# A two-layer graph attention kernel: the bias products taken out of the matrix engine, the biases added to stored rows, and one normalisation moved from VectorE to ScalarE

## The chip, the cores and the metric

The kernel runs on one core of one Trainium2 chip. The metric is the device time of one execution in microseconds (us); shorter is better. The core has five engines with a queue each: TensorE (PE in the profile, with its weight loads as PEld), VectorE (DVE), ScalarE (ACT), GpSimd (POOL) and SyncE (SP). Transfers are issued from the queues of SP, ACT and POOL and are carried by 16 DMA engines.

## The reference

A graph has 3125 nodes with 768 features and 53125 edges, sorted by destination (two directions of 25000 edges, and one loop per node). The reference adds one more loop per node inside each layer.

```
h  = relu(layernorm(x))
# layer 1: 4 heads of 256 columns
xl = h @ W1
e  = leaky_relu((xl . a_src)[src] + (xl . a_dst)[dst], 0.2);  alpha = softmax of e over the edges of one dst
g  = sum over edges (xl[src] * alpha) + b1
h1 = relu(layernorm(g) * g1 + be1) + (h @ Wr1 + br1)
# layer 2: one head of 768 columns
g  = sum over edges ((h1 @ W2)[src] * alpha2) + b2
out = x + layernorm(g) * g2 + be2 + (h1 @ Wr2 + br2)
```

The weights alpha of one node add up to 1. A vector added to every row of `xl` therefore comes out of the weighted sum unchanged.

## The kernel before

The nodes are cut into NB = 25 blocks of P = 125. The edges that end in one block fill a window of S = 2304 slots, J = 18 tiles of 128 slots. `in_order` (line 59) is the part that runs; `any_order` serves unsorted edges. The work has four stages.

**Stage 1, to about 515 us.** A loop over the blocks of x (line 683) does for each: `stats` (bn_stats on DVE, square root on ACT), `normal` (line 607, in place on the tile `xt`), `flip` (PE transposes, relu on ACT), and `fetch` of a later block of x into one of AHEAD = 8 `xt` tiles (line 590, from POOL's queue from block 4 on). Beside it run `edge_list`, `windows` and the folding of the attention vectors into W1 (lines 308 and 309), all on DVE. The generator `products` (line 637) multiplies each block by W1; ACT copies the two halves out of PSUM into `row` (line 648) and POOL's queue stores the row to `table1` (line 651). `split_biases` (line 155) splits b1, b2 and br2 + be2 into a high and a low part, and stores both in DRAM as `parts_d`. Then `softmax` (line 333) computes the weights of layer 1 for all windows: for each block it loads the destinations and sources of the window to all partitions (`bd`, `bs`, lines 370 and 372), turns them into one-hot matrices on DVE (`ohd`, `ohs`), picks rows by PE products, and reduces on DVE; steps of `products` fill PE between. What is left of `products`, and the first residual product (line 744), close the stage.

**Layer 1, to about 1511 us.** `sums` (line 486) goes through the blocks, 18 tiles each. For one tile, POOL gathers 128 rows of `table1` by an indirect DMA into `g` (line 525), one of ten buffers. In 17 of 18 tiles ACT writes `hi = g * alpha` rounded (line 543), DVE writes the remainder back into `g` (line 544), and PE multiplies both by a one-hot matrix made by DVE (lines 536 and 548) and adds up in the PSUM tile `pa`. In the remaining tile the weights go into the one-hot matrix, and PE works on full float32 (line 560). After the last tile of a block, two matmuls over two rows add the bias: `ones_r` by `b1_r`, high and low part (line 564); they are the last that write `pa`. Then `finish` (line 502) adds the row of the extra loop on DVE (line 512), and `end1` (line 793) runs spread over the next block's tiles: bn_stats, square root on ACT, normalisation on DVE (line 798), PE transposes, relu with g1 and be1 on ACT, the residual added on DVE, sixteen PE products with W2 (line 820), ACT copies the two halves of the row out of PSUM (line 824), DVE copies two attention columns (line 826), and SP stores the row to `table2`. The residual products of layer 1 (line 777) are spread between the tiles as well.

**The weights of layer 2, to about 1690 us.** `softmax` again, with `residual` (line 848) as filler on PE: sixteen products with Wr2 per block, then two matmuls that add br2 + be2 (line 858), then DVE adds the block of x (line 863). The first nine blocks are done here.

**Layer 2.** `sums` with one head of 768 columns and 18 buffers for `g`; 13 of 18 tiles are split, five use weights in the one-hot matrix. The two matmuls of line 564 add b2. The other 16 blocks of `residual` are spread over the tiles. `end2` normalises and adds, and ACT's queue stores the result.

The order on PE is as written in the source in all stages, that on ACT and DVE in stage 1's loop and in both calls of `sums`. Elsewhere, and on POOL and SP, a scheduler orders the instructions when the program is built. Each queue runs in its order, so an instruction that waits holds up what stands behind it.

The functions that the change touches, and what calls them:

Of the kernel before, what the change touches and what calls it, by code (L numbers as in the profile page):

```python
# [28 lines left out]
J = 18  # L29
# [29 lines left out]
def in_order(  # L59
# [45 lines left out]
    parts_d = dram.tile([2, HC + 2 * C2], F32, name="parts_d")  # L105
# [49 lines left out]
    def split_biases(pool):  # L155

        for name, vec, plus, n, o in (("b1", b1, None, HC, 0), ("b2", b2, None, C2, HC), ("ball", br2, be2, C2, HC + C2)):
            v = pool.tile([128, n // 128], F32, name=name + "_v")
            nc.sync.dma_start(v, vec.rearrange("(p c) -> p c", p=128))
            if plus is not None:  # L160
                u = pool.tile([128, n // 128], F32, name=name + "_u")
                nc.sync.dma_start(u, plus.rearrange("(p c) -> p c", p=128))
                nc.vector.tensor_add(v, v, u)
            hi = pool.tile([128, n // 128], F32R, name=name + "_hi")
            nc.vector.tensor_copy(hi, v)
            lo = pool.tile([128, n // 128], F32R, name=name + "_lo")
            nc.vector.tensor_sub(lo, v, hi.bitcast(F32))
            for i, t in enumerate((hi, lo)):
                nc.sync.dma_start(parts_d[i, o:o + n].rearrange("(p c) -> p c", p=128), t.bitcast(F32))

    def bias_rows(pool, o, n, name):
        t = pool.tile([2, n], F32R, name=name)
        nc.sync.dma_start(t.bitcast(F32), parts_d[:, o:o + n])
        return t

# [3 lines left out]
    def divided(pool, v, shape, name, by=P):  # L179

        t = pool.tile(shape, F32, name=name + "t")
        nc.vector.tensor_scalar(t, v, 1.0 / by, -0.5 + 0.5 / by, op0=OP.mult, op1=OP.add)
        ti = pool.tile(shape, I32, name=name + "i")
        nc.vector.tensor_copy(ti, t)
        q = pool.tile(shape, F32, name=name + "q")
# [3 lines left out]
        up = pool.tile(shape, F32, name=name + "u")  # L189
# [62 lines left out]
    def windows(pe):  # L252

        with tc.tile_pool(name="wn", bufs=1) as ep:
# [22 lines left out]
            q, _ = divided(ep, src_s, [128, NB * J], "sh")  # L277
# [55 lines left out]
    def softmax(heads, asad, al, alo_d, pp, nq, ends=False, scr=None, fill=iter(()), side=None,  # L333
# [8 lines left out]
        with tc.tile_pool(name="so", bufs=1, side=side, reuse_waits=waits) as so:  # L342
# [8 lines left out]
            with tc.tile_pool(name="sb", bufs=2, side=side, reuse_waits=waits) as sb:  # L351
# [16 lines left out]
                for b in range(NB):  # L368
# [3 lines left out]
                    bs = sb.tile([128, S], I16, name="bs", bufs=2)  # L372
# [6 lines left out]
                    ohs = sb.tile([128, S], BF16, name="ohs")  # L379
# [36 lines left out]
            with tc.tile_pool(name="sr", bufs=1, side=side, reuse_waits=waits) as sr:  # L416
# [5 lines left out]
                s = sr.tile([128, J, heads, NB], F32, name="s")  # L422
# [63 lines left out]
    def sums(heads, cols, table, al, alo_d, bias, split, ahead, his, lag, gp, pp, end, more=iter(())):  # L486
# [6 lines left out]
        assert split(0) or n == f  # L493
        running = []
# [21 lines left out]
        with tc.manual_schedule(engines={PE, ACT, DVE}) if lag else nullcontext():  # L516
            for b in range(NB):
# [3 lines left out]
                for j in range(J):  # L521
# [15 lines left out]
                    if split(j):  # L537
# [8 lines left out]
                        for t in (hi, g):  # L546
                            for i in range(2):
                                nc.tensor.matmul(pa[:, i, :f], oh[:, :P], t[:, i * f:(i + 1) * f],  # L548
                                                 start=(j == 0 and t is hi), stop=False)
# [12 lines left out]
                    if j == J - 1:  # L562
                        for i in range(2):
                            nc.tensor.matmul(pa[:, i, :f], ones_r, bias[:, i * f:(i + 1) * f],  # L564
                                             start=False, stop=True)
# [6 lines left out]
    with tc.tile_pool(name="m1", bufs=1) as mp:  # L572
# [10 lines left out]
        with tc.tile_pool(name="w1", bufs=1) as wp, tc.tile_pool(name="pm1", bufs=1, space=PSUM) as pm1:  # L583
            w1 = wp.tile([128, NK1, HC], F32, name="w1")
            wa1 = wp.tile([128, NK1, 2 * H], F32, name="wa1")
            h0 = []
            with tc.tile_pool(name="d1", bufs=2) as dp, tc.tile_pool(name="pd1", bufs=1, space=PSUM) as pp:
                xts = {}

# [47 lines left out]
                def products():  # L637

                    for b in range(NB):
                        gi, o = b // GB, (b % GB) * P  # L640
                        row = wp.tile([P, HC], F32, name="row", bufs=2)
                        for i in range(2):
                            pm = pm1.tile([128, 512], F32, name="pm", bufs=3)
                            for k in range(NK1):
                                nc.tensor.matmul(pm[:P], h0[gi][:, k, o:o + P], w1[:, k, i * 512:(i + 1) * 512],  # L645
                                                 start=(k == 0), stop=(k == NK1 - 1))
                                if k == NK1 - 1:
                                    nc.scalar.activation(row[:, i * 512:(i + 1) * 512], pm[:P], AF.Copy)  # L648
# [27 lines left out]
                with tc.manual_schedule(engines={ACT, DVE}):  # L676
# [6 lines left out]
                    for b in range(-2, NB + LAG):  # L683
                        if b + 2 < NB:
                            stats(b + 2)
                        if b == -1:

                            nc.vector.memset(w1[:, :, 0:HC:512], 0.0)
                            for i in range(2):
# [4 lines left out]
                                fetch(5 + 2 * i)  # L694
# [20 lines left out]
            with tc.tile_pool(name="pq1", bufs=1, space=PSUM) as pp:  # L715
# [6 lines left out]
                split_biases(mp)  # L722
# [27 lines left out]
        with tc.tile_pool(name="w2", bufs=1, reuse_waits="tile") as wp, tc.tile_pool(name="e1", bufs=2, reuse_waits="tile") as ep, \  # L750
# [12 lines left out]
            b1_r = bias_rows(wp, 0, HC, "b1_r")  # L763
# [29 lines left out]
            def end1(b, z):  # L793
# [4 lines left out]
                nc.vector.tensor_scalar(z, z, mu, rstd, op0=OP.subtract, op1=OP.mult)  # L798
# [30 lines left out]
            sums(H, C1, table1, al1, alo1_d, b1_r, lambda j: j % 18 != 8, 10, 4, 0, gp, pp, end1, later())  # L829


    with tc.tile_pool(name="m2", bufs=1, reuse_waits="tile") as mp, \
            tc.tile_pool(name="pr2", bufs=1, space=PSUM, reuse_waits="tile") as pr:
        al2 = mp.tile([128, J, 1, NB], F32, name="al2")
        ball_r = bias_rows(mp, HC + C2, C2, "ball_r")
# [4 lines left out]
        def load(b):  # L840
            if b < NB and b not in loaded:
# [58 lines left out]
        with tc.tile_pool(name="w3", bufs=1, reuse_waits="tile") as wp, tc.tile_pool(name="e2", bufs=2, reuse_waits="tile") as ep, \  # L900
                tc.tile_pool(name="g2", bufs=1, reuse_waits="tile") as gp, tc.tile_pool(name="pg2", bufs=1, space=PSUM, reuse_waits="tile") as pp:
            b2_r = bias_rows(wp, HC, C2, "b2_r")
# [12 lines left out]
            with tc.issue_after(behind):  # L915
                sums(1, C2, table2, al2, alo2_d, b2_r, lambda j: j % 18 not in (0, 4, 8, 12, 16), 18, 10, 5, gp, pp, end2, more)
# [472 lines left out]
```

## Time and profile before

| what | value |
|---|---|
| median of 15 executions | 2363.51 us (2354.13 to 2371.64) |
| the profiled execution's own time | 2368.95 us |
| its span, first to last instruction | 2367.1 us |
| mean granted PE clock | 0.974 |
| PE busy | 2213.1 us, 93% |
| DVE busy | 1975.8 us, 83% |
| ACT busy | 1295.1 us, 55% |
| POOL busy | 1197.3 us, 51% |
| moved by DMA | 637.97 MB, 270 GB/s on average |

The profile shows one execution. "Busy" counts an engine's time in instructions, waits left out. The span is also cut into 40 equal slices of some 59 us with the busy share of each in tenths. A group row gives line, engine, operation, output and inputs with their shapes, the count, busy us, the mean ns of one, and the idle time of the engine just before with what ended it. The chain of waits is followed back from the last instruction: at each step to what released it. A timeline row begins with start and length in us.

### The profile page before, as it was taken

The page shows a single profiled execution, that of the slowest core. Times are in us where ns is not written, and L with a number is a line of the kernel's source. Part 1 is how long each engine was busy: PE and PEld are TensorE (multiplying, and loading weights), DVE is VectorE, ACT ScalarE, POOL GpSimd, SP SyncE. Part 2 cuts the span into 40 slices and gives each one's busy share as a digit, 9 for nine tenths or more (in the row PEclk, how much of TensorE's full clock was granted, in tenths as well). Part 3 has the DMA queues.
Part 4 walks back from the last instruction along what each step waited for, and adds up shares of the span by engine and source line. Part 5 has one row for each costly group of instructions (what it writes and reads, how often), then busy time and mean ns, then how long its engine had stood idle before and what let it go on. Part 6 is the DMA issues. An engine that isn't in the chain of part 4 may idle for free.

```text
span 2367.1 us, 35889 instructions
## 1 busy us (share of the span) xinstructions
PE 2213.1 (93%) x11154; PEld 1436.0 (61%) x11154; DVE 1975.8 (83%) x4429; ACT 1295.1 (55%) x2687; POOL 1197.3 (51%) x1043
## 2 busy tenths in 40 slices
PE   5898999989999999999999999799999999999997
PEld 2566665436666666666666765476566666666664
DVE  6845999769999999898989999588678787778877
ACT  1222332229988888888888999100244444444443
POOL 2100000027765666655556776000377777777775
PEclk8898999989999999999999999899999999999999
DMA  5453552379998898988988998686499999898896
GB/s 185 147 190 103 182 192 87 112 237 376 336 324 304 288 340 296 314 314 287 332 289 295 335 319 291 243 292 236 157 316 331 331 321 316 312 310 309 299 308 226
DMA packets 185691, 637.97 MB, mean 270 GB/s; under 512 B 32170, under 2 KB 49435, under 8 KB 184724
## 3 DMA queue, kind: packets, MB, share of 16 engines
q0 software_dynamic: 109072, 437.23, 54.0%
q1 hardware_dynamic: 72570, 188.75, 22.7%
q10 hardware_dynamic: 3850, 9.60, 1.1%
q8 instruction: 93, 1.52, 0.2%
q14 instruction: 106, 0.87, 0.1%
HBM read 567.40 MB, written 68.08 MB: 268 GB/s over the span
## 4 chain that ended last, share of the span: by engine, by line
PE 59%; DVE 21%; DMA 12%; issue 3%; ACT 3%; POOL 1%; SPq 0%; ACTq 0%; DVEq 0%; POOLq 0%
PE pa L548 18%; PE p L820 10%; DMA g<-table,idx_s 9%; PE pr L777 7%; PE pr L854 6%; PE pm L645 5%; PE pa L560 5%; DVE g L544 5%; ACT hi L543 2%; DVE scr L394 2%; DVE al L397 2%; PE pq L392 2%; PE pm L744 2%; PE pas L633 1%; PE pa L564 1%
## 5 line engine op out<-in xcount | busy, mean ns | idle before, releaser
L525 POOL DMA_INDIRECT g<-table,idx_s x900 | 1088.9, 1210 | 485.8 <-PE pa L548 284.3
L543 ACT ACTIVATE hi<-g,al 128x256 fp32r<-128x256 f32 (+1 forms) x2025 | 1009.1, 575 | 469.8 <-DMA g<-table,idx_s 281.8
L544 DVE SCALAR_TENSOR_TENSOR g<-g,al,hi 128x256 fp32r<-128x256 f32 (+1 forms) x2025 | 1032.7, 560 | 131.9 <-ACT hi L543 130.3
L548 PE MATMUL pa<-hi,oh 128*125 128x512 f32 (+1 forms) x1500 | 602.8, 481 | 25.3 <-DVE oh L536 18.2
L548 PE MATMUL pa<-g,oh 128*125 128x512 f32 (+1 forms) x1500 | 473.8, 391 | 24.1 <-DVE g L544 23.8
L548 PEld LDWEIGHTS pa<-hi,oh 128*125 128x125 f32 x1500 | 273.6, 188 | 218.2 <-ACT hi L543 71.1
L548 PEld LDWEIGHTS pa<-g,oh 128*125 128x125 f32 x1500 | 270.8, 187 | 109.6 <-DVE g L544 67.4
L820 PE MATMUL p<-w,h1T 128*125 128x384 f32 (+1 forms) x800 | 299.9, 493 | 2.2 <-DVE h1T L811 1.9
L854 PE MATMUL pr<-wr,h 128*125 128x384 f32 x800 | 294.1, 500 | 3.8 <-DMA h<-h1T_d 3.2
L645 PE MATMUL pm<-w,h 128*125 128x512 f32 x600 | 283.7, 623 | 0.0
L777 PE MATMUL pr<-h0k,wr 128*128 128x500 f32 (+1 forms) x576 | 257.7, 536 | 10.3 <-DMA h0k<-h0T_d 10.2
L536 DVE TENSOR_SCALAR oh<-iota_f,rel_s 128x128 fp32r<-128x128 f32 x775 | 207.4, 279 | 60.3 <-PE pa L548 60.2
L560 PE MATMUL pa<-g,w 128*125 128x384 f32 (+1 forms) x700 | 235.0, 464 | 5.7 <-ACT w L558 4.8
L854 PEld LDWEIGHTS pr<-wr,h 128*125 128x125 f32 x800 | 149.8, 192 | 85.9 <-issue 13.5
L820 PEld LDWEIGHTS p<-w,h1T 128*125 128x125 f32 x800 | 148.4, 188 | 81.4 <-issue 10.9
L146 POOL DMA_DIRECT2D table<-row x25 | 15.8, 631 | 347.4 <-ACT row L648 320.4
L645 PEld LDWEIGHTS pm<-w,h 128*125 128x125 f32 x600 | 113.8, 197 | 126.7 <-issue 126.4
L560 PEld LDWEIGHTS pa<-g,w 128*125 128x125 f32 x700 | 129.2, 190 | 72.1 <-ACT w L558 15.0
L777 PEld LDWEIGHTS pr<-h0k,wr 128*128 128x128 f32 x576 | 104.5, 191 | 53.3 <-issue 11.5
L392 PEld LDWEIGHTS <-ohs 125*128 125x128 bf16 x2700 | 101.2, 98 | 48.3 <-DVE ohs L380 33.8
L392 PE MATMUL pq<-tabs,ohs 125*128 125x100 bf16 (+1 forms) x2700 | 104.9, 192 | 22.9 <-DVE ohs L380 21.1
L648 ACT ACTIVATE row<-pm 125x512 f32<-125x512 f32 x50 | 29.8, 595 | 150.9 <-PE pm L645 138.6
(198 smaller groups left out, 1681.8 us busy)
## 6 DMA issues: line engine op xcount, KB each, us to landing
bd<-dst_d SPq DMA_DIRECT2D x50, 576.0 KB
bs<-slo_d SPq DMA_DIRECT2D x50, 576.0 KB
g<-table,idx_s POOLq DMA_INDIRECT x900, 6.1
r1T_d<-rt SPq DMA_DIRECT2D x100, 125.0 KB
r1t<-r1T_d SPq DMA_DIRECT2D x25, 500.0 KB
h1T_d<-h1T SPq DMA_DIRECT2D x25, 500.0 KB
h<-h1T_d SPq DMA_DIRECT2D x25, 500.0 KB
own<-table SPq DMA_DIRECT2D x24, 512.0 KB
```

Of the source, the lines that this page charges most:

```text
L392: nc.tensor.matmul(q[:, j], ohs[:P, (j0 + j) * 128:(j0 + j + 1) * 128], tabs[:, i], start=(i == 0), stop=(i == 2))
L394: nc.vector.tensor_tensor(pick[:, j0:j0 + n], q, ohh[:, j0:j0 + n, None, :].to_broadcast([128, n, heads, NB]), OP.mult)
L525: nc.gpsimd.indirect_dma_start(out=gf, out_offset=None, in_=table[:, :], in_offset=bass.IndirectOffsetOnAxis(ap=idx_s[:, c:c + 1], axis=0))
L536: nc.vector.tensor_scalar(oh, iota_f, rel_s[:, c:c + 1], None, op0=OP.is_equal)
L543: nc.scalar.activation(hi[:, cs], gf[:, cs], AF.Copy, scale=a)
L544: nc.vector.scalar_tensor_tensor(g[:, cs], gf[:, cs], a, hi[:, cs].bitcast(F32), op0=OP.mult, op1=OP.subtract)
L548: nc.tensor.matmul(pa[:, i, :f], oh[:, :P], t[:, i * f:(i + 1) * f], start=(j == 0 and t is hi), stop=False)
L560: nc.tensor.matmul(pa[:, o // f, o % f:o % f + n], w[:, o // cols, :], gf[:, o:o + n], start=(j == 0), stop=False)
L645: nc.tensor.matmul(pm[:P], h0[gi][:, k, o:o + P], w1[:, k, i * 512:(i + 1) * 512], start=(k == 0), stop=(k == NK1 - 1))
L777: nc.tensor.matmul(pm[:, :nb * P], wr1[:, k, m * 128:(m + 1) * 128], loaded[gi, k][:, :nb * P], start=(k == 0), stop=(k == NK1 - 1))
L820: nc.tensor.matmul(pm[:, :n], hT[:, k, :], w2[:, k, o:o + n], start=(k == 0), stop=(k == NK2 - 1))
L854: nc.tensor.matmul(pm[:, :384], h1[:, k, :], wr2[:, k, i * 384:(i + 1) * 384], start=(k == 0), stop=False)
```

## The change

- The matmuls over two rows (lines 564 and 858), `split_biases`, `bias_rows` and the DRAM tensor `parts_d` go. The last product of a block carries the stop mark instead.
- b1 is added by GpSimd to each row of table 1 in SBUF, after ACT's copies and before the store.
- b2 is added by VectorE while it takes the row of table 2 out of PSUM; the two ScalarE copies there go.
- br2 + be2 is added by GpSimd to x, block by block, in stage 1 (`plus`); the sum is stored to DRAM as `xb_d`, and layer 2 loads it in place of x. `plus` reads `xt` before `normal` writes over it. b1, br2 and be2 are loaded, broadcast to 125 partitions, from ACT's queue.
- The normalisation of layer 1 (line 798) becomes an ACTIVATE with scale and bias; DVE makes the bias from mean and inverse deviation first.
- To make room: 7 `xt` tiles instead of 8; the one-hot matrix `ohs` is written over `bs`, of which there are 3 (layer 1) or 4 (layer 2) instead of 2; `s` is written over `m`; four tiles of a division share one.

```diff
-    parts_d = dram.tile([2, HC + 2 * C2], F32, name="parts_d")
+    xb_d = dram.tile([N, D], F32, name="xb_d")
...
-                    bs = sb.tile([128, S], I16, name="bs", bufs=2)
+                    bs = sb.tile([128, S], I16, name="bs", bufs=3 if scr else 4)
...
-                    ohs = sb.tile([128, S], BF16, name="ohs")
+                    ohs = bs.bitcast(BF16)
...
-                s = sr.tile([128, J, heads, NB], F32, name="s")
+                s = m
...
                                 nc.tensor.matmul(pa[:, i, :f], oh[:, :P], t[:, i * f:(i + 1) * f],
-                                                 start=(j == 0 and t is hi), stop=False)
+                                                 start=(j == 0 and t is hi),
+                                                 stop=(j == J - 1 and t is g))
...
-                    if j == J - 1:
-                        for i in range(2):
-                            nc.tensor.matmul(pa[:, i, :f], ones_r, bias[:, i * f:(i + 1) * f],
-                                             start=False, stop=True)
...
+            b1_b = wp.tile([P, HC], F32, name="b1_b")
+            nc.scalar.dma_start(b1_b, bcast(b1, HC))
...
+                ball_b = dp.tile([P, D], F32, name="ball_b", bufs=1)
+                nc.scalar.dma_start(ball_b, bcast(br2, D))
+
+                def plus(b):
+
+                    xb = dp.tile([P, D], F32, name="xb", bufs=XB)
+                    if b == 0:
+                        nc.scalar.dma_start(xb, bcast(be2, D))
+                        nc.gpsimd.tensor_add(ball_b, ball_b, xb)
+                    nc.gpsimd.tensor_add(xb, xts[b][:P], ball_b)
+                    store_rows(nc.gpsimd, xb_d, b, xb)
...
+                                        nc.gpsimd.tensor_add(row, row, b1_b)
                                         store_rows(nc.gpsimd, table1, b, row)
...
-                AHEAD, LAG = 8, 10
+                AHEAD, LAG, XB = 7, 10, 2
...
                         if 0 <= b + 1 < NB:
+                            if b == -1:
+                                plus(0)
+                                plus(1)
+                            if b + 3 < NB:
+                                plus(b + 3)
                             normal(b + 1)
...
-                split_biases(mp)
...
-            b1_r = bias_rows(wp, 0, HC, "b1_r")
+            b2_b = wp.tile([P, C2], F32, name="b2_b")
+            nc.sync.dma_start(b2_b, bcast(b2, C2))
...
-                nc.vector.tensor_scalar(z, z, mu, rstd, op0=OP.subtract, op1=OP.mult)
+                off = ep.tile([P, 1], F32, name="off")
+                nc.vector.tensor_scalar(off, mu, rstd, -1.0, op0=OP.mult, op1=OP.mult)
+                nc.scalar.activation(z, z, AF.Identity, bias=off, scale=rstd)
...
-                    nc.scalar.activation(row[:, o:o + 384], pm[:, :384], AF.Copy)
+
+                    nc.vector.tensor_add(row[:, o:o + 384], pm[:, :384], b2_b[:, o:o + 384])
...
-                load_rows(nc.sync, xr, x, b)
+                load_rows(nc.sync, xr, xb_d, b)
...
-                                     start=(k == 0), stop=False)
+                                     start=(k == 0), stop=(k == NK2 - 1))
                 yield
-            for i, pm in enumerate(pms):
-                nc.tensor.matmul(pm[:, :384], ones_r, ball_r[:, i * 384:(i + 1) * 384], start=False, stop=True)
```

More of the change, by code (lines that the diff above doesn't have):

```diff
@@ L153, in by_chunk, with divided @@
         return t
[L155 to L174, printed above, removed]
     def start_of(b):
         return nc.values_load(starts[0:1, b:b + 1], engines=[SP], min_val=0, max_val=E - S)
-    def divided(pool, v, shape, name, by=P):
-        t = pool.tile(shape, F32, name=name + "t")
+    def divided(pool, v, shape, name, by=P, room=None):
+        if room is None:
+            room = [pool.tile(shape, F32, name=name + x) for x in "tiqu"]
+        t, ti, q, up = room
+        ti = ti.bitcast(I32)
         nc.vector.tensor_scalar(t, v, 1.0 / by, -0.5 + 0.5 / by, op0=OP.mult, op1=OP.add)
-        ti = pool.tile(shape, I32, name=name + "i")
         nc.vector.tensor_copy(ti, t)
-        q = pool.tile(shape, F32, name=name + "q")
         nc.vector.tensor_copy(q, ti)
         nc.vector.scalar_tensor_tensor(t, q, -float(by), v, op0=OP.mult, op1=OP.add)
-        up = pool.tile(shape, F32, name=name + "u")
         nc.vector.tensor_scalar(up, t, float(by), None, op0=OP.is_ge)
@@ L276, in windows @@
             yield
-            q, _ = divided(ep, src_s, [128, NB * J], "sh")
+            room = ep.tile([128, 4, NB * J], F32, tag="tf", name="room")
+            q, _ = divided(ep, src_s, [128, NB * J], "sh", room=[room[:, i, :] for i in range(4)])
             nc.vector.tensor_copy(hi_s, q)
@@ L484, in softmax, with sums @@
         return behind
-    def sums(heads, cols, table, al, alo_d, bias, split, ahead, his, lag, gp, pp, end, more=iter(())):
+    def sums(heads, cols, table, al, alo_d, split, ahead, his, lag, gp, pp, end, more=iter(())):
         width = heads * cols
@@ L493, in sums @@
         assert split(0) or n == f
+        assert split(J - 1)
         running = []
@@ L693, in in_order @@
                                 fetch(4 + 2 * i)
-                                fetch(5 + 2 * i)
+                                if i == 0:
+                                    fetch(5)
                         if b == 1:
@@ L827, in end1 @@
                 store_rows(nc.sync, table2, b, row)
-            sums(H, C1, table1, al1, alo1_d, b1_r, lambda j: j % 18 != 8, 10, 4, 0, gp, pp, end1, later())
+            sums(H, C1, table1, al1, alo1_d, lambda j: j % 18 != 8, 10, 4, 0, gp, pp, end1, later())
     with tc.tile_pool(name="m2", bufs=1, reuse_waits="tile") as mp, \
@@ L834, in in_order @@
         al2 = mp.tile([128, J, 1, NB], F32, name="al2")
-        ball_r = bias_rows(mp, HC + C2, C2, "ball_r")
         FIRST = 9
@@ L901, in in_order @@
                 tc.tile_pool(name="g2", bufs=1, reuse_waits="tile") as gp, tc.tile_pool(name="pg2", bufs=1, space=PSUM, reuse_waits="tile") as pp:
-            b2_r = bias_rows(wp, HC, C2, "b2_r")
             g2_b = wp.tile([P, C2], F32, name="g2_b")
@@ L915, in in_order @@
             with tc.issue_after(behind):
-                sums(1, C2, table2, al2, alo2_d, b2_r, lambda j: j % 18 not in (0, 4, 8, 12, 16), 18, 10, 5, gp, pp, end2, more)
+                sums(1, C2, table2, al2, alo2_d, lambda j: j % 18 not in (0, 4, 8, 12, 16), 18, 10, 5, gp, pp, end2, more)
 @with_exitstack
```

## The prediction, on record before the result

> **What bounds the kernel now.** I read the slices first, then busy time by stretch, then the chain of waits in each stretch. A stretch row gives its length, busy us (and instructions) of PE, PEld, DVE, ACT and POOL, the granted clock, the DMA share and GB/s.
>
> ```profile
> PE   5898999989999999999999999799999999999997
> DVE  6845999769999999898989999588678787778877
> DMA  5453552379998898988988998686499999898896
> ...
> 40.00:100.00 60.00, 49.50 (x152) 25.12 (x152) 58.28 (x113) 13.44 (x34) 9.35 (x16) 0.89 0.38 125
> ...
> 300.00:385.00 85.00, 81.57 (x970) 54.03 (x971) 84.59 (x120) 29.42 (x31) 6.23 (x10) 1.00 0.50 161
> ...
> 600.00:800.00 200.00, 199.61 (x717) 129.08 (x716) 185.90 (x520) 173.40 (x433) 129.94 (x101) 1.00 0.90 315
> ...
> 1700.00:1900.00 200.00, 189.45 (x731) 129.50 (x731) 159.51 (x314) 94.64 (x108) 155.91 (x145) 0.99 0.92 320
> ```
>
> Four bounds follow each other. From 33 to 95 us and from 210 to 425 us DVE sets the pace (58.3 of 60, 84.6 of 85). In layer 1 it is PE (199.6 of 200), with DVE close behind at 93%. In layer 2 it is PE and the gathers in turn: between 1700 and 2300 us the chain of waits lies 29.5% on the gather's DMA and about 44% on PE (lines 548, 854, 560, 564), and ACT waits 248.0 us of 600 for gathered rows.
>
> **What goes from PE.** The price of a bias pair is read from starts, since matmul records overlap.
>
> ```profile
> 789.07 0.62 PE L548 MATMUL pa<-g,oh 128*125 128x512 f32 x2
> 789.54 1.45 PE L820 MATMUL p<-w,h1T 128*125 128x384 f32 x4
> ...
> 792.14 0.63 PE L548 MATMUL pa<-g,oh 128*125 128x512 f32 x2
> 792.70 0.72 PE L564 MATMUL pa<-b_r,ones_r 2*125 2x512 f32 x2
> 793.35 1.56 PE L820 MATMUL p<-w,h1T 128*125 128x384 f32 x4
> ```
>
> From line 548 to line 820 it takes 0.47 us without the pair and 1.21 with it: 0.74 us, 25 times, 18.5 us in layer 1. In layer 2 the same reading (1801.42 to 1802.39, against 1807.56 to 1807.91) gives 0.62 us: 25 pairs of line 564 are 15.5 us, 16 of line 858 are 9.9. In the second softmax line 854's four records and the pair take 2.02 us (1569.34 to 1571.36) against 1.33 for four records: 0.69 us, nine times, 6.2 us. Together 50.1 us; the two groups' busy time is 33.4 + 15.2 = 48.6, so the reading holds.
>
> **Layer 1: take -15.** A block takes 39.67 us (line 564 at 633.18 and 672.85) and PE is full, so up to 18.5 us come. DVE loses the normalisation (25 x 0.912 = 22.8) and gains 50 row adds out of PSUM at 546 ns (line 863, 125x384, same shape and places: 27.3) and 25 `off` at about 154 ns (line 327's reciprocal: 3.9): +8.4, or 0.33 a block. It then has 37.2 us of work in blocks of 38.9, 96%. ACT loses 24.6 (line 824) and gains 25 ACTIVATEs on 1024 elements, which I estimate at 1.03 us from 512 elements in 595 ns (line 648) and 2304 in 2123 (line 378): 25.8. New is a wait: ACT's normalisation waits for DVE's `off`, with the next tile's `hi` queued behind it, for which DVE and then PE wait. Four `hi` buffers lie between (ACT waits 71.0 us for PE from 560 to 1400, so they are mostly full). From 18.5 I take off 3.5 for this. If that cover fails, ACT's 1.03 us and DVE's 0.56 ahead of it come back in each block, and nothing is left.
>
> **Second softmax: -6.** PE is busy 84.8 of 87 us there, so nearly all comes; at worst, where DVE is last, nothing. `bs` no longer waits for DVE two blocks back but for PE's products four blocks back, long done; the order on SP is the same. I cost that at nothing; SP's row, if it did wait, would hold `bd` too.
>
> **Layer 2: -11.** Of 25.4 us only what lies on PE's part of the chain counts: 44% is 11. Ends: 0, if the DMA engines (0.92 busy) have no more to give, and 25. `xr` is loaded from `xb_d` instead of x, same size and queue.
>
> **Stage 1, its start: take +4.** DVE's queue stands still today for the split biases:
>
> ```profile
> 20.30 0.59 DVE L220 TENSOR_SCALAR_CACHE_REDUCE less<-d 125x425 bf16<-125x425 int16 x1
> ...
> 32.17 0.17 DVE L165 CAST b_hi<-b_v 128x8 fp32r<-128x8 f32 x1 [11.27 <-DMA b_v<-in_L_gnn_b_dram]
> ```
>
> This wait and some 1.0 us of small instructions go. What is late next: `normal` of block 0, today at 6.22 us, now waits for `plus(0)`, which in POOL's queue stands behind all twelve loads of W1 and another of x. Today these are issued by 20.7 us, each waiting for an earlier one to land. ACT's three broadcasts add 1.26 MB; at the 299 GB/s of the first 20 us that is 4.2 us. Then two GpSimd adds on 768 elements. Their price is in no row of this trace. POOL's select on 128x128 took 283 ns; in proportion to the elements 768 take 1.70 us and 1024 take 2.26, my upper end. DVE's TENSOR_TENSOR on 1024 took 1.217 us (line 308) and on 768 0.946 (line 736), my lower end. I take the upper, the row of the engine itself. So `normal(0)` starts near 20.7 + 4.2 + 3.4 = 28.3, DVE needs 10.3 us of work to the place where it stood, and 38.6 replaces 33.2 (32.17 and the 1.0): +5. Lower end, no delay of transfers and fast adds: 22.6 + 10.3 - 33.2 = -0.3. Upper end +8, if the adds are late again for the next blocks (two `xb` tiles, each bound to its store). I take +4.
>
> **Stage 1, GpSimd beside DVE: take +12.** 25 adds on 768 and 25 on 1024 elements come onto POOL, whose queue is nearly empty in time (9.4 us busy of the 60 shown), so their own time is hidden; the last lies under line 744's 40 us. But they may hold up DVE where it is the bound. A row shows that the two do meet:
>
> ```profile
> 285.77 1.19 POOL L146 DMA_DIRECT2D table<-row  x1 [18.32 <-ACT row L648]
> 286.04 0.80 DVE L375 TENSOR_SCALAR ohd<-bd,node_f 128x2304 bf16<-128x2304 int16 x1
> 286.95 0.51 POOL L147 DMA_DIRECT2D table<-row  x1
> ```
>
> An issue that takes 0.536 us in the median takes 1.19 beside a fast VectorE instruction. In DVE's two stretches stand about ten `plus` and four row adds, then eleven row adds: 10 x 1.70 + 15 x 2.26 = 51 us. Ends: 0, if they do not disturb DVE, and 51, if each stops it in full. DVE instructions with two SBUF operands or of the fast kind fill 46% of a folding round (2 x 1.22 + 0.62 of 6.69 us) and 41% of a softmax block (3.0 of 7.3), and part of each meeting falls on others: I take a quarter, 12 us.
>
> [...] The row above shows POOL as the loser; no row shows DVE losing. [...]
>
> **Sum.** -15 - 6 - 11 + 4 + 12 = -16, from the profiled execution's 2368.95 us (span 2367.1) to 2353. That execution lies 5.4 us above the median of 2363.5, so the same change to the median is 2347.5, my forecast.
>
> **Rivals.**
>
> - *The adds cost nothing.* For it: POOL is idle, and the wait of 11.27 us goes. Then -18.5 - 6.2, 60% of layer 2's 25.4 (-15) and 0: -40, 2324.
> - *The next engine takes over.* DVE at 96% and ACT's new wait keep layer 1 at -6, the gathers (0.92 of the DMA engines, 29.5% of the chain) keep layer 2 at -3, softmax -6, against +15: 2363.5, no change. Against it: the four `hi` buffers.
> - *GpSimd paces stage 1 (the slower one).* Place: DVE's stretches from 33 to 95 and 210 to 425 us. Price: 51 us in full. From a loss of 28 there, over half of each add, beside +4 and the gains of 32, the change stops paying. With 51 + 8 - 32 it is +27, 2390. For it: DVE has no slack there; against: most DVE time in the softmax goes to reductions and to instructions with an operand in PSUM.
>
> **Numbers.** Forecast 0.45 (own range 2335 to 2357), adds free 0.20, next engine 0.17, GpSimd as the bound 0.18. Faster by over 0.2% (4.7 us, what a measurement can tell from no change): 0.45 + 0.20 + 0.03 of the third = 0.68; same 0.14; slower 0.18. The range 2322 to 2372 takes in the first three and leaves out most of the last.
>
> **What would show it.** Layer 1's block of 39.67 us should come to 39.0; DVE near 95% there, and no longer PE waits for ACT. `normal(0)` should start at 26 to 30 us. Lines 308, 375, 380 and 382 should show longer or later instances beside POOL's adds; if the DVE-bound stretches keep their lengths, the quarter is wrong. Layer 2's blocks should shrink by 0.4 us of some 26; by 1.0 or by 0 the chain's shares misled me. The forecast fails if the adds last over 3 us, or ACT's wait for `off` empties the `hi` buffers.

## The result: slower by 2.8%, and the profile after

The changed kernel takes 2430.49 us (median of 9 executions, 2417.84 to 2436.3) against 2362.67 (47 executions): a ratio of 1.0278, with an interval of 1.0261 to 1.0295, and +68 us between the medians. Its profiled execution has 2421.39 us with a span of 2419.5, +52.4 to the span of before. The rest lies between executions: the profiled one is 9.1 us below its median, that of before 6.3 above.

The slices after, against those shown of before:

```profile
PE   2789888898899999999999998889899999998996
DVE  4983899877899999999999999767778878888887
DMA  6454454148999898899898989588289999998987
```

PE starts late (2 where there was 5), and the part up to layer 1 fills about one slice more. The stretches that answer to the four shown of before: folding, first softmax, layer 1, layer 2.

```profile
61.00:121.00 60.00, 45.87 (x130) 22.70 (x129) 58.11 (x76) 10.31 (x27) 41.01 (x40) 0.87 0.49 156
340.00:425.00 85.00, 75.27 (x872) 49.33 (x869) 85.00 (x109) 28.57 (x29) 15.32 (x12) 0.98 0.48 165
660.00:860.00 200.00, 195.45 (x696) 126.77 (x694) 183.97 (x524) 173.75 (x427) 139.13 (x104) 0.99 0.90 317
1750.00:1950.00 200.00, 183.06 (x701) 126.89 (x700) 155.97 (x307) 93.23 (x105) 155.62 (x145) 0.97 0.92 321
```

The first of these begins with the `pe<-cnt` product, which ends the start; the row of before at 40:100 begins 6 us ahead of it, among short instructions. From `pe<-cnt` on, before has:

```profile
46.10:106.10 60.00, 52.62 (x184) 28.63 (x185) 55.30 (x99) 13.73 (x35) 9.02 (x15) 0.87 0.42 139
```

In the first two, DVE is as full as before or fuller but gets less done: 76 instructions in 60 us where there were 99, 109 in 85 where there were 120. That is how a slowed engine looks: busy, with fewer and longer instructions. POOL went from 9.02 to 41.01 in the first.

Starts of the same instructions cut the span into stretches (us); the last ends with the last `z`. The other columns are experiments below, all from chips on which before took 2362 to 2367 us.

| stretch, to | before | after | e_no_plus | e_no_rowadd | e_neither | e_dma_b1 |
|---|---|---|---|---|---|---|
| `pe<-cnt` product | 46.1 | 60.7 | 51.5 | 59.9 | 45.6 | 37.5 |
| last folding reduction | 47.4 | 63.3 | 51.7 | 55.3 | 47.4 | 47.5 |
| first `pq` product | 115.3 | 124.1 | 113.7 | 117.9 | 115.7 | 118.5 |
| first scan | 187.6 | 201.2 | 201.4 | 186.1 | 186.3 | 190.4 |
| third scan | 29.7 | 34.6 | 34.6 | 30.0 | 29.7 | 30.3 |
| second softmax (layer 1) | 1086.8 | 1082.4 | 1078.9 | 1095.9 | 1095.5 | 1060.0 |
| its first scan | 126.8 | 132.0 | 128.4 | 131.7 | 126.1 | 125.5 |
| its third scan | 22.4 | 23.5 | 21.2 | 23.6 | 22.4 | 22.4 |
| last `z` (layer 2) | 699.2 | 691.9 | 697.7 | 694.5 | 694.8 | 699.1 |
| ratio to before | 1 | 1.0278 | 1.0105 | 1.0174 | 1.0036 | 0.988 |

Up to layer 1 the change loses 57.8 us (14.6 + 15.9 + 8.8 + 13.6 + 4.9); all after that gains 5.4, where the forecast had 32.

The start, in the timeline of after (POOL, then DVE):

```profile
29.29 0.54 POOL L140 DMA_DIRECT2D xt<-in_x_dram  x1 [1.02 <-DMA xt<-in_x_dram]
29.85 1.81 POOL L579 TENSOR_TENSOR ball_b<-ball_b,xb 125x768 f32<-125x768 f32 x1
31.74 3.56 POOL L580 TENSOR_TENSOR xb<-xt,ball_b 125x768 f32<-125x768 f32 x2
...
33.58 2.14 DVE L605 TENSOR_SCALAR xt<-xt,bn_mv,bn_rs 125x768 f32<-125x768 f32 x1 [23.00 <-POOL xb L580]
```

DVE's wait of 11.27 us went, and one of 23.00 came: the last load ahead of the adds is issued at 29.29. `normal` itself takes 2.14 us where it took 0.68 in before, with the second `plus` beside it.

The folding's products, as groups by line within their stretch, before and after:

```profile
L308 DVE TENSOR_TENSOR ab<-w,ab 128x1024 f32<-128x1024 f32 x12 | 14.6, 1217 | 0.0
```

```profile
L288 DVE TENSOR_TENSOR ab<-w,ab 128x1024 f32<-128x1024 f32 x12 | 26.3, 2192 | 0.0
L289 DVE TENSOR_REDUCE wa<-ab 128x4 f32<-128x1024 f32 x11 | 13.4, 1220 | 0.4
...
L580 POOL TENSOR_TENSOR xb<-xt,ball_b 125x768 f32<-125x768 f32 x8 | 17.4, 2181 | 0.1
L644 POOL TENSOR_TENSOR row<-row,b_b 125x1024 f32<-125x1024 f32 x3 | 8.2, 2736 | 15.7 <-ACT row L641 15.7
```

The twelve products with two SBUF operands take 11.7 us more, the reductions between them exactly what they took. DVE as a whole is not slower; some of its instructions are held. In the first softmax it is the three comparisons of 16-bit tiles, again before and after, from first `pq` to first scan:

```profile
L375 DVE TENSOR_SCALAR ohd<-bd,node_f 128x2304 bf16<-128x2304 int16 x23 | 18.5, 803 | 0.0
L380 DVE TENSOR_SCALAR ohs<-bs,node_f 128x2304 bf16<-128x2304 int16 x23 | 18.4, 802 | 0.0
L377 DVE TENSOR_SCALAR scr<-bd,node_f 128x2304 bf16<-128x2304 int16 x21 | 16.8, 801 | 0.0
```

```profile
L355 DVE TENSOR_SCALAR ohd<-bd,node_f 128x2304 bf16<-128x2304 int16 x23 | 26.4, 1147 | 0.0
L357 DVE TENSOR_SCALAR scr<-bd,node_f 128x2304 bf16<-128x2304 int16 x21 | 20.3, 966 | 0.0
L360 DVE TENSOR_SCALAR bs<-bs,node_f 128x2304 bf16<-128x2304 int16 x22 | 19.4, 884 | 0.0
...
L644 POOL TENSOR_TENSOR row<-row,b_b 125x1024 f32<-125x1024 f32 x9 | 24.2, 2685 | 161.1 <-ACT row L641 161.1
```

They take 66.1 us in place of 53.7: 12.4 of the stretch's +13.6. One meeting in the timeline of after:

```profile
261.60 2.34 POOL L644 TENSOR_TENSOR row<-row,b_b 125x1024 f32<-125x1024 f32 x1 [21.45 <-ACT row L641]
...
262.23 2.33 DVE L355 TENSOR_SCALAR ohd<-bd,node_f 128x2304 bf16<-128x2304 int16 x1
```

POOL's add ends at 263.94; `ohd` ends at 264.56, 0.62 us later. Alone it takes 0.80 us, so it got nearly nothing done beside the add. Each of the nine row adds of this stretch met such an instruction: four `ohd`, three `scr`, one `bs`, and one small instruction on `room` (2.22 us). The second scan of each pair loses 2.1 us (7.04 against 4.93), also beside a row add; before and after:

```profile
401.22 4.93 DVE L454 TENSOR_TENSOR_SCAN bw<-pen,scr 100x2304 f32<-100x2304 bf16 x1
...
454.12 7.04 DVE L435 TENSOR_TENSOR_SCAN bw<-pen,scr 100x2304 f32<-100x2304 bf16 x1
```

### The profile page after: what moved, and what is told of

The parts are those of the page before. It is cut to its first block, busy times and chain, and to the rows that moved or that the text cites. A ratio compares the mean times of both kernels' runs of the same rounds, so it can differ in the third digit from the quotient of the medians.

```text
span 2419.5 us, 35744 instructions
## 1 busy us (share of the span) xinstructions
PE 2189.8 (91%) x11004; PEld 1437.1 (59%) x11004; DVE 2037.8 (84%) x4472; ACT 1299.1 (54%) x2662; POOL 1367.3 (57%) x1144
## 4 chain that ended last, share of the span: by engine, by line
PE 54%; DVE 23%; DMA 14%; issue 4%; ACT 3%; POOL 1%; SPq 1%; ACTq 0%; DVEq 0%; POOLq 0%
PE pa L530 17%; DMA g<-table,idx_s 10%; PE p L822 9%; PE pr L777 7%; PE pr L856 5%; PE pm L638 5%; DVE g L526 5%; PE pa L543 4%; ACT hi L525 2%; DVE scr L374 2%; DVE al L377 2%; PE pm L743 2%; PE pq L372 2%; PE pas L626 1%; DVE z L494 1%
## 5 line engine op out<-in xcount | busy, mean ns | idle before, releaser
L507 POOL DMA_INDIRECT g<-table,idx_s x900 | 1111.8, 1235 | 460.2 <-PE pa L530 243.8
L530 PE MATMUL pa<-g,oh 128*125 128x512 f32 (+1 forms) x1500 | 485.6, 397 | 32.0 <-DVE g L526 31.4
L638 PE MATMUL pm<-w,h 128*125 128x512 f32 x600 | 291.0, 636 | 0.0
L644 POOL TENSOR_TENSOR row<-row,b_b 125x1024 f32<-125x1024 f32 x25 | 66.9, 2677 | 285.8 <-ACT row L641 285.8
L372 PEld LDWEIGHTS <-bs 125*128 125x128 bf16 x2700 | 102.4, 98 | 62.3 <-DVE bs L360 47.9
L372 PE MATMUL pq<-tabs,bs 125*128 125x100 bf16 (+1 forms) x2700 | 106.3, 193 | 35.4 <-DVE bs L360 32.6
L641 ACT ACTIVATE row<-pm 125x512 f32<-125x512 f32 x50 | 29.8, 596 | 187.4 <-PE pm L638 161.0
```

The lines of the kernel that those rows point to most:

```text
L372: nc.tensor.matmul(q[:, j], ohs[:P, (j0 + j) * 128:(j0 + j + 1) * 128], tabs[:, i], start=(i == 0), stop=(i == 2))
L507: nc.gpsimd.indirect_dma_start(out=gf, out_offset=None, in_=table[:, :], in_offset=bass.IndirectOffsetOnAxis(ap=idx_s[:, c:c + 1], axis=0))
L644: nc.gpsimd.tensor_add(row, row, b1_b)
```

## The experiments

**Theory:** GpSimd's adds hold up DVE where DVE sets the pace, and `plus` makes the start late. **Rival:** the changed rooms (`ohs` over `bs`, `s` in `m`, seven `xt`) slow stage 1. The chips are not alike: before took 2362 to 2413 us on them, with layer 2 alone 30 to 40 us longer on the slower ones, and layer 1 differs between them too. So each kernel is compared with runs of before on its own chip, by the ratio; the stretches on DVE agree between chips (folding 47.4 us in each kernel without adds).

**The parts undone one by one.**

```diff
-  nc.gpsimd.tensor_add(xb, xts[b][:P], ball_b); store_rows(nc.gpsimd, xb_d, b, xb)   # e_no_plus, e_neither
+  ball_r pair in residual(), xr from x
-  nc.gpsimd.tensor_add(row, row, b1_b)                                               # e_no_rowadd, e_neither
+  b1_r pair in layer 1
```

Where a pair comes back, so does the split of its bias at the start, and DVE's wait for it (10.9 us in `e_no_plus`, 10.7 in `e_neither`, 24.5 in `e_no_rowadd`, where `plus` stands at the start too).

> The changed kernel, but br2 + be2 are not added to x by GpSimd: they come back as the bias pair in the second softmax (hi and lo split on VectorE, two columns into the product), and xr is loaded from x. The row adds of b1 stay. Theory 1 (GpSimd's adds hold VectorE up, and plus(0) makes the start late): the 14.6 us of the late start and the 15.9 us that the folding stretch lost come back, less up to 6 us for the pair in the second softmax: 2395 to 2408 us, and the VectorE group of line 288 (2192 ns mean in the changed kernel, 1217 before) falls to below 1.4 us in its instances before 95 us. Rival (the shared buffers, the shorter list of fetches and the s = m room slow stage 1): 2425 to 2437.

Ratio 1.0105 (1.0069 to 1.0141), 2386.71 us: more came back than expected (1.7%). The folding took 51.7 us, its twelve products 1462 ns each, a little above the 1.4 expected: three row adds still stand beside them.

> The changed kernel, but b1 is not added to the rows by GpSimd: it comes back as the bias pair in layer 1's 25 blocks. plus stays. Theory 1 (GpSimd's adds hold VectorE up): the softmax loop's +16 us and the folding rounds' share of it go, but up to 18.5 us for 25 pairs come back in layer 1, of which the changed kernel gained only 6: 2405 to 2422 us, with the first softmax's blocks at 5.8 to 8.0 us and no ohd instance above 1.3 us between 245 and 440 us. Rival (the rooms): 2430 to 2450, the softmax's blocks stay uneven.

Ratio 1.0174 (1.0126 to 1.0221); 2407.07 us, as expected. Softmax and scans are back at 186.1 and 30.0, and the longest `ohd` takes 0.90 us where it took 2.92; layer 1 is at 1095.9, with the pair and the rest of the change.

> The changed kernel without either GpSimd add: b1 and br2 + be2 are bias pairs again; b2 on VectorE out of PSUM, layer 1's normalisation on ScalarE and all rooms stay as changed. Theory 1: stage 1 is as long as before the change (last reduction of the first softmax at 380 to 390 us), layer 2 keeps its 6 us or more: 2350 to 2362 us. Rival (the rooms slow stage 1): 2385 to 2415.

Ratio 1.0036 (1.0019 to 1.0053); 2374.65 us, 13 above the theory's upper end, on a chip where before took 2367.18. Stage 1 is as before in each stretch, as expected, but layer 1 is 8.7 us longer and layer 2 only 4.4 shorter. So of the 2.8% the adds cost 2.4, net of the pairs that they save and of the wait for their split, and the remaining parts of the change do not pay either.

> The kernel before with the changed rooms alone: bs with 3 or 4 buffers, ohs written over bs, s in the room of m, seven xt tiles in place of eight and the fetch of tile 5 alone moved; all bias products as before. Theory 1: 2360 to 2367 us, no change. Rival (the rooms slow stage 1): 2385 to 2420.

Ratio 0.9998 (0.9981 to 1.0015). The rival falls.

**What about the adds costs: their place, the rows' longer way, or SBUF?** On `e_neither`, an add or a set that touches no row:

```diff
+  nc.gpsimd.tensor_add(pad, pad, pad)   # e_scratch_add; e_scratch_set: nc.gpsimd.memset(pad, 1.0)
   store_rows(nc.gpsimd, table1, b, row)
```

> The kernel without GpSimd adds (e_neither, 2374.7 us), but at the place of each row add GpSimd adds a tile of 125 x 1024 of its own to itself: no one waits for it but the row's store behind it in POOL's queue, and it touches no row. The computation is otherwise that of e_neither. [...] Rival A, the cost is that of the row's way (ScalarE's row held longer by the add, its store later): 2370 to 2379, stretch 185 to 188.

If the adds' reads are what costs, the price was to be 15 to 25 us over `e_neither`, in the softmax stretch (first `pq` product to first scan, the stretch of these expectations), which would take 198 to 203. Ratio 1.0150 (1.0116 to 1.0184) against 1.0036, some 27 us: about that price, but not in that place. As nothing tied the adds to their rows, the scheduler put 23 of them into the folding, which grew from 47.4 to 71.2 us, while the softmax stretch stayed at 185.7. The groups within the folding:

```profile
L309 DVE TENSOR_TENSOR ab<-w,ab 128x1024 f32<-128x1024 f32 x12 | 27.0, 2250 | 0.0
...
L617 DVE TENSOR_SCALAR xt<-xt,bn_mv,bn_rs 125x768 f32<-125x768 f32 x7 | 10.8, 1540 | 0.3
...
L656 POOL TENSOR_TENSOR pad<-pad 125x1024 f32<-125x1024 f32 x23 | 51.6, 2243 | 1.4
```

Of the 23.8 us, the products took 12.4. `normal` took 6.0 (1.54 us in the mean where 0.68 is usual), so an instruction on float32 with one SBUF tensor is held as well.

> The same, but GpSimd sets its own 125 x 1024 tile to a constant: it writes SBUF and reads nothing. Theory 1 with the narrow rule (only reads meet VectorE's second operand; a write meets only the fast forms): 2374 to 2382 us, the stretch at 186 to 191, and the TENSOR_TENSOR group with two SBUF inputs (ohh, 1.5 us) unchanged beside a set while ohd and ohs may be longer. Rival B, any use of SBUF by GpSimd holds VectorE up: per microsecond of GpSimd as dear as e_scratch_add.

Ratio 1.0058 (1.0035 to 1.0081), folding 48.6 us (`ohh`, put at 1.5 us in the expectation, takes 0.61 in before). The same place, POOL writing only:

```profile
L309 DVE TENSOR_TENSOR ab<-w,ab 128x1024 f32<-128x1024 f32 x12 | 14.6, 1214 | 0.0
...
L656 POOL MEMSET pad<- 125x1024 f32 x24 | 23.8, 993 | 1.0
```

No data passes between the two engines in either kernel; 51.6 us of adds that read cost 23.8 us, 23.8 us of writes 1.2. An add alone takes 1.90 us here, so each cost DVE 1.03 us, 54% of it.

The softmax stretch had still to be tried with the row's way kept and its reads taken away:

```diff
-  nc.gpsimd.tensor_add(row, row, b1_b)
+  nc.gpsimd.memset(row, 1.0); nc.gpsimd.memset(row, 1.0)   # on e_no_plus
```

> The changed kernel with br2 + be2 as a bias pair (e_no_plus, 1.0105 of before), and at each row add's place GpSimd sets the row twice to a constant instead of adding b1: it waits for the row, holds it about 1.9 us and delays its store as the add (2.34 us) does, but reads no SBUF. The table of layer 1 then holds a constant, so the outputs are not the reference's. [...] Rival A (the row's longer way and its late store): stretch 198 to 202, ratio 1.008 to 1.011.

If only the adds' reads cost, the stretch to the first scan was to come back to 186 to 189 us, the scans' to 30 and the ratio to 1.000 to 1.003. Ratio 1.0015 (0.9998 to 1.0032), and the scans are back at 30.6; but the stretch to the first scan took 194.9, between that and the rival's. Its groups:

```profile
L381 DVE TENSOR_SCALAR bs<-bs,node_f 128x2304 bf16<-128x2304 int16 x22 | 21.7, 985 | 0.0
L376 DVE TENSOR_SCALAR ohd<-bd,node_f 128x2304 bf16<-128x2304 int16 x23 | 19.4, 846 | 0.0
L378 DVE TENSOR_SCALAR scr<-bd,node_f 128x2304 bf16<-128x2304 int16 x21 | 19.0, 904 | 0.0
```

The comparisons take 60.1 us, 6.4 above before, of +7.3 for the stretch. So the row's way without reads costs half of the 13.6, and most of that is again time in which DVE's comparisons are held. A set holds up the 16-bit comparisons too (0.85 to 0.99 us in the mean beside sets, 0.80 in before), though not products with two SBUF operands: they take 1214 ns beside sets (`e_scratch_set`), 2250 beside adds (`e_scratch_add`) and 1217 in before.

**The start.**

```diff
+  plus(0); plus(1)                 # ahead of W1's twelve loads in POOL's queue
   nc.gpsimd.dma_start(w1[...], W1[...])
```

> The changed kernel (2430.5 us) with plus(0) and plus(1) ahead of W1's twelve loads in POOL's queue, and the broadcast of b1 behind those of br2 and be2. Theory 2, the late start is the wait behind W1's loads: normal(0) moves from 33.6 us to about 14 to 18, the product pe<-cnt from 60.7 to 48 to 52, and 8 to 13 us of the whole go: 2417 to 2423. If the adds themselves and not their place make the start late: 2426 to 2433, normal(0) above 26 us.

Ratio 1.0250 (1.0214 to 1.0285), not told apart from the change's. `normal(0)` moved to 26.8 only, and `pe<-cnt` came at 64.6, later than in after. DVE's timeline:

```profile
26.80 2.14 DVE L605 TENSOR_SCALAR xt<-xt,bn_mv,bn_rs 125x768 f32<-125x768 f32 x1 [16.13 <-POOL xb L580]
...
42.73 2.15 DVE L605 TENSOR_SCALAR xt<-xt,bn_mv,bn_rs 125x768 f32<-125x768 f32 x1 [9.59 <-POOL xb L580]
```

23.00 us of waiting became 16.13 + 9.59: with the adds first, the first waits for the broadcast of be2 (landed at 22.6), and the third `plus` stands behind W1. The theory's figures fail; `normal(0)` above 26 us, as the other side had it, holds. The wait belongs to a chain of load, add and in-place `normal`, not to one place in the queue.

**The parts of layer 1 alone, on before.**

```diff
-  nc.scalar.activation(row[:, o:o + 384], pm[:, :384], AF.Copy)             # e_b2_only, and no b2_r pair
+  nc.vector.tensor_add(row[:, o:o + 384], pm[:, :384], b2_b[:, o:o + 384])
-  nc.vector.tensor_scalar(z, z, mu, rstd, op0=OP.subtract, op1=OP.mult)     # e_norm_only
+  nc.scalar.activation(z, z, AF.Identity, bias=off, scale=rstd)
```

> The kernel before with one part of the change: b2 is added by VectorE as it takes the rows for layer 2 out of PSUM, b2's pair in layer 2 goes. Normalisation stays on VectorE, b1 and br2 + be2 stay bias pairs. e_neither was 8.7 us longer than before from the scans to the last product of layer 1 and 4.5 shorter in layer 2. If VectorE's 50 row adds (27 us onto an engine at 93%) cost layer 1 that: layer 1 +6 to +15 here and the whole 2368 to 2378 us. If ScalarE's normalisation, which now waits for VectorE's off, costs it: layer 1 within 3 us of before, the whole 2358 to 2364.

Ratio 1.0067 (1.0043 to 1.0090): against before on the same chip, b2 on VectorE loses, although its pair in layer 2 is gone. Where is less clear. From the first to the last `z`, layer 1 takes 942.3 us, where before takes 931.3 on another chip. But `e_scratch_set`, on the chip of `e_b2_only`, takes 942.2 where `e_neither`, with the same layer 1, takes 933.9 on another. So these 11.0 us cannot be put down to the row adds. A block takes 39.7 us (median) in both kernels.

> The kernel before with one part of the change: layer 1's normalisation on ScalarE with VectorE's off, all biases as before. If VectorE's row adds alone cost layer 1 its +8.7 us, this takes 25 x 0.76 us off VectorE and leaves layer 1 (second pair of scans to the last product) at 1080 to 1088 us: ratio 0.996 to 1.001. If ScalarE's wait for off costs: layer 1 at 1090 to 1096, ratio 1.002 to 1.005.

Ratio 0.9993 (0.9974 to 1.0011): by itself it is worth nothing. First to last `z` take 932.5 us, against 929.6 on the same chip in `e_early_bias` below, whose layer 1 is that of before. Both parts together cost little between the first and the last `z`: on one chip, 933.9 in `e_neither` against 932.1 in `e_rooms`. Of the 10.0 us by which layer 1 is longer in `e_neither` than in `e_rooms`, 6.2 lie ahead of the first `z`, where no row add has run yet. From the third scan to the first `z`, nine of ten kernels with b2 on VectorE take 135 to 139 us (one takes 131), the five without 123 to 133. The broadcast of b2 (375 KB) now stands among layer 1's loads in SP's queue; whether it is the cause was not tried.

**The second softmax.** In after, `keep` is late, and in SP's queue g2's broadcast of 375 KB now stands ahead of it (SP and DVE, before and after):

```profile
1632.69 0.28 SPq L424 DMA_DIRECT2D keep<-keep_d  x1
...
1633.33 0.26 SPq L904 DMA_DIRECT2D g_b<-in_L_gnn_g_dram  x1
...
1638.80 0.75 DVE L426 TENSOR_SCALAR pen<-keep 25x2306 bf16<-25x2306 bf16 x1 [0.58 <-DMA keep<-keep_d]
```

```profile
1686.24 0.33 SPq L903 DMA_DIRECT2D g_b<-in_L_gnn_g_dram  x1
1687.58 0.27 SPq L405 DMA_DIRECT2D keep<-keep_d  x1
...
1697.31 0.75 DVE L407 TENSOR_SCALAR pen<-keep 25x2306 bf16<-25x2306 bf16 x1 [4.84 <-DMA keep<-keep_d]
```

```diff
-  nc.sync.dma_start(keep, keep_d[:R, :])
+  (nc.scalar if side else nc.sync).dma_start(keep, keep_d[:R, :])
```

> The changed kernel with one line moved: in the second softmax, keep is loaded from ScalarE's queue and no longer stands in SP's queue behind g2's broadcast. If that place is what made VectorE wait 4.84 us for keep ahead of the second softmax's scans: the wait falls below 1.5 us, first pq product to first scan of the second softmax from 132.0 to 127 to 129, ratio 1.024 to 1.027. If the DMA engines' load is the cause and not the queue: wait above 3 us, ratio 1.026 to 1.030.

Ratio 1.0224 (1.0197 to 1.0252); the wait fell to 2.81 us, but the stretch took 136.5, where three kernels with the pair took 129.8 to 133.9 on that chip. ScalarE issued `keep` only at 1694.54, after g2's broadcast (1690.46), so the edit did not bring the load forward: inconclusive.

The kept profiles say more of the order. The load of b2's vector, which stood between the two in before, does not decide it: `e_no_plus`, `e_neither`, `e_b2_only` and three more kernels have no such load either, and there `keep` is first and DVE does not wait for it. Of the kernels that load `keep` from SP's queue, g2 stands first only in after, `e_no_rowadd` and `e_plus_first`, all with `plus` and `xb_d`; there DVE waits 4.84, 5.44 and 0.95 us. On one chip the stretch to the first scan takes 131.7 in `e_no_rowadd`, and 128.4 and 126.1 in `e_no_plus` and `e_neither`. So `plus` is what goes with the late `keep`; that the order in the queue makes the wait is likely but not shown.

**A version that beats both.**

```diff
-  nc.sync.dma_start(v, vec.rearrange("(p c) -> p c", p=128))      # e_early_bias, on before
+  nc.scalar.dma_start(v, vec.rearrange("(p c) -> p c", p=128))
...
+  store_rows(nc.sync, table1, b, b1_b)                            # e_dma_b1: b1 into all rows first,
+  nc.gpsimd.dma_start(table1[rows of b], row, accum_op=OP.add)    # the row added on the way; no b1_r
```

> The kernel before with one line moved: the four loads of b1, b2, br2 and be2 for the split go to ScalarE's queue, ahead of its first work, in place of SP's queue behind the edge list's store. VectorE's wait of 11.27 us at 20.9 us goes, as the change promised it, and nothing is added to GpSimd. If VectorE's order is the bound from there on: pe<-cnt moves from 46 to 35 to 38 us and the whole loses 5 to 11 us, ratio 0.995 to 0.998. If W1's or x's loads are late next: pe<-cnt 40 to 45, ratio 0.998 to 1.001.

Ratio 0.9950 (0.9932 to 0.9967): `pe<-cnt` at 33.4, below the expected 35. This is the gain that the change was to have at the start, without `plus`.

> e_early_bias (ratio 0.995) with b1 in the table's rows as the change has it, but not by GpSimd's arithmetic: the table is first filled with b1's broadcast by 25 stores, and the rows' stores from POOL's queue add to what lies there in the DMA itself; layer 1's 25 pairs go; the changed rooms, b2 and br2 + be2 as before the change. If the loss in stage 1 was GpSimd's operand reads and the gain of b1's pair in layer 1 is real: fold 47 us, first pq product to first scan 186 to 188, first to last product of layer 1 shorter by 11 to 16 us than with the pair (941 to 948 in place of 951.7 from the second scans' first p product on), ratio 0.988 to 0.991. If the adding stores slow the stage (their read and write of HBM, the fill's 12.8 MB): ratio 0.993 to 1.003 with the stage's lengths up. If the layer gives the pair's time back to VectorE or the gathers: 0.994 to 0.996.

Ratio 0.9880 (0.9860 to 0.9900), 2336.33 us against 2362.20: the fastest of all. The folding stays at 47.5; the softmax stretch, at 190.4, is 2.4 above the expected. From first to last `z` layer 1 takes 914.9 in place of 931.3 (-16.4), a block 38.8. These two profiles need not be of one chip; on one chip `e_no_plus`, without b1's pair, takes 918.1, and `e_neither`, with it, 933.9: -15.8. Another 9.9 us come before the first `z`, where PE waited 10.2 us for the reloaded `h0k` and now waits 1.5; why these land sooner was not tried. POOL only issues; its groups in the softmax stretch:

```profile
L655 POOL DMA_DIRECT2D table<-row x9 | 11.3, 1259 | 0.0
L654 POOL DMA_DIRECT2D table<-row x9 | 9.8, 1089 | 170.2 <-ACT row L651 170.2
```

## Why the prediction was wrong

The forecast was 2347.5, 16 us below the median of 2363.5; the median became 2430.49, 67 above. The third rival, GpSimd as the bound, happened, given 0.18. Even its 2390 was too low, because it kept the gains of 32 us, of which 5.4 came.

- **GpSimd beside DVE, +12: the step that failed** is "part of each meeting falls on others: I take a quarter". No row of before shows which of DVE's instructions an add holds: that it is those in the 46% and the 41%, and the quarter, were the author's estimates. In after the folding's products (1217 to 2192 ns in the mean), the comparisons (0.80 to between 0.88 and 1.15 us), `normal` in the folding (0.68 to 0.86) and the second scan (4.93 to 7.04) were held, the reductions (1220 ns) were not. In the two stretches that it counted, folding, softmax and scans lost 15.9 + 13.6 + 4.9 = 34.4 us of the 51, two thirds in place of a quarter; the stretch between them, not counted, lost 8.8 more. In the folding DVE waited for no one: the products (+11.7), one small product (+2.4) and `normal` (+1.2) make up nearly all of it. Measured cleanly, an add cost 54% of its time (`e_scratch_add`), and nine row adds of 2.34 us, 21.1, cost 13.6 in the softmax, 65%. The share of vulnerable time in DVE's mix is the wrong measure, because the meetings are not drawn at random. While DVE is held it stands in the vulnerable instruction, so it loses all that is left of the add (the comparisons in eight of the nine meetings end 0.61 to 0.62 us behind the add); and such instructions follow each other so closely that all nine row adds met one. The scans, with two SBUF operands, were not in the shares, nor was `normal`. In the stretch of 8.8 us, thirteen `normal` took 17.7 us in place of 8.8, but DVE also waits some 46 us for PE there, and kernels without any add vary from 112.5 to 118.5; how much of the 8.8 the adds make is left open.
- **The start, +4:** became +14.6. The mechanism was right, the size was not. `normal(0)` started at 33.6 in place of 28.3, because the loads ahead of the adds had left POOL's queue at 29.8 and not at 24.9. Another 3.9 us came behind it, where DVE was held by `plus` (2.14 us in place of 0.68 for the first `normal`, some more for later ones) and waited for it again (1.23). That the wait passes from block to block came out of `e_plus_first`.
- **Layer 1, -15:** its mechanism was right. A block went from 39.7 to 39.0 as forecast. On one chip, first to last `z` took 918.1 in `e_no_plus` against 932.1 in `e_rooms`, -14.0; in the profiled execution of after only 7.6 came, where one early block took 44.1 us. What was not in the sum lies ahead of the first `z`: 137.2 us in `e_no_plus` against 131.2 in `e_rooms`. DVE's row adds, put down as fitting into 96%, left the block as it was (39.7 in `e_b2_only`), but that kernel as a whole lost 0.7%.
- **Second softmax, -6:** became +6.3. PE busy 84.8 of 87 us did not make PE the bound: the loop takes 120.1 us with the pairs and 121.7 without, and PE's share simply fell (87.8 to 85.7 us of 90 within it). `bs` and `bd` were rightly costed at nothing (126.0 us to the first scan in `e_rooms`). What the forecast did not look at is the load of `keep` behind the loop, late by 4.3 us in after.
- **Layer 2, -11:** -7.3, with -1.5 to -4.7 in the three kernels beside it. The chain's share gave too much; why was not tried.

## What to carry to other kernels

An idle engine is not free if it meets the one that sets the pace. Look whether the busy engine's instructions are of the kinds that were held here (in after, products with two SBUF operands: 1.22 us alone and up to 4.23; 16-bit comparisons: 0.80 and up to 2.92; `normal` on float32: 0.68 and up to 2.75), and cost each add beside them at half to two thirds of its own time, as measured here (54% and 65%), not at a share of the mix. A bias can be added by the store itself, without arithmetic on any engine (`e_dma_b1`, ratio 0.9880). When loads are added, moved or taken out, read the new order of their queue in the profile: here a broadcast came to stand ahead of the one transfer that was waited for.

## What the runs showed of the hardware

- GpSimd setting 125x1024 floats (0.99 us in the mean of `e_scratch_set`) leaves DVE's products of two SBUF operands alone (1214 ns against 1217), but lengthens 16-bit comparisons (0.80 to between 0.85 and 0.99 us in the mean of `e_row_set`).
- The loss is mutual: in after, the row add takes 2.34 us alone and 2.69 in the mean of the softmax stretch.
- A GpSimd add leaves DVE's reductions alone (1220 ns with adds and without, in the folding), but holds `normal` on float32 (0.68 us, up to 2.75 in after).
- A store that adds in the DMA costs POOL 1.1 to 1.3 us to issue in the mean of the softmax stretch, where a plain one took 0.54 to 0.80, and 12.8 MB of extra fill; with both, no stretch of the stage behind the start is longer than in before by more than 3.2 us.
